# A transformer block on one core: the last block's end taken by quarters, tiles and two engines, score units by heads, and steps reordered at both ends

## The chip, the cores and the metric

One core of a Trainium2 chip runs the whole program. The metric is the device time of one execution in microseconds (us). TensorE (PE) multiplies matrices, VectorE (DVE), ScalarE (ACT) and GpSimd (POOL) work on tiles in SBUF and PSUM, and SyncE (SP) issues nearly all DMA transfers, in its own order.

## What is computed

A transformer block with adaptive norms over x of shape (8, 1024, 512), 16 heads of 32 columns, an MLP of width 2048, all in float32:

```python
mod = silu(condition) @ Wada + bada
sh_a, sc_a, gt_a, sh_m, sc_m, gt_m = split(mod, 6, axis=1)
xm = layernorm(x, g1, be1) * (1 + sc_a) + sh_a
x  = x + gt_a * (causal_attention(xm, Wqkv) @ Wproj + bproj)
xm = layernorm(x, g2, be2) * (1 + sc_m) + sh_m
x  = x + gt_m * (gelu(xm @ W1 + b1) @ W2 + b2)
```

## The kernel before, in words

The 8 x 1024 tokens are 16 blocks of 512 (two for each sequence); block n is the even or odd half of sequence n // 2. Two streams of work are merged into each engine's queue by a planner written in Python, which runs when the program is built and keeps a clock for each engine (`now`, L94), the time at which each value is ready (`written`) and the time at which each buffer is free (`left`).

The **attention stream** is `attend()` (L1392). For block n and each group g of 4 heads it runs *weight units* (`weights_T` L1282: transposed scores less the row maximum on PE into the PSUM tile "st", exponent on ACT L1317, on POOL the causal select L1322; then `weigh` L1334, the product with v, L1345) and, for the group that follows, *score units* (`scores` L1196: scores on PE into the same "st", L1208, causal mask L1220 and row maxima L1228 on DVE). An even block has 3 weight and 3 score units a group, an odd one 7 and 7. The exponents are added up in place over a group on POOL (L1429). `finish` (L1355) sums them over partitions by a matmul (L1363), copies the sums (L1369), takes their reciprocals on DVE in four parts (L1378) and divides on POOL (L1383). With the last group of a block this sets "attended" for it.

The **linear stream** is a generator that runs the steps of `plan` (L228 to L264) in order: k, q, v (projections for later blocks), "proj" (output projection, `project_out` L844), "mt" (norm, modulation and transposes ahead of the MLP, `modulated` L579), u (four up parts), d (four down parts, `down` L914; part 0 to 3 hold 2, 2, 1 and 2 products). Products are done by Strassen-like schemes with weight sums that are made once at the start: for W1 and W2 by `preparation()` (L670), stage by stage, four loads, four in-place additions on DVE or POOL (`either`, L148), four stores. "proj" of block n waits for "attended" n; "mt" is started as a side thread beside the main one. `work()` (L1106) advances the thread that can go soonest, the first of equals, side threads standing ahead of the main one:

```python
def threads():
    return sides + ([main] if main[0] is not None else [])
...
    advance(min(threads(), key=lambda thread: wait_of(thread[1])))
```

`step_aside` (L1135) stands ahead of each attention unit: it lets linear work in while that unit would have to wait, or while linear work is behind its share (`stream`). DVE work that isn't urgent (reciprocals, norm statistics) lies in `jobs`, and work that needs another ACT table (the norm's root and scaling L552 to L569, the gelu L871) in `excursions`; these run at set places of `attend`, or when `work()` finds every thread blocked.

Weights come through a ring of 9 tiles (`fetch`, L321), loaded by SP in the order in which the plan uses them; loads of x (L1035), gate rows (L489) and stores (L911) are issued in the same queue.

At the end (window 16, L264) the plan is: load x, down part 2 of block 14, proj 15, down part 3 of block 14, mt 15, and the MLP of block 15. The last down part of block 15 has its two products, then gate (POOL or DVE), addition and the two stores.

Of the kernel before, what the change touches and what calls it, by code (L numbers as in the profile page):

```python
# [22 lines left out]
def kernel(  # L23
# [123 lines left out]

    def either(out, a, b, op, reads, writes):  # L148

        n = 1  # L150
        for d in out.shape[1:]:
            n *= d
        on_dve, on_pool = 60 + 1.24 * n, 120 + 2.28 * n
        t = due(reads, writes)
        if max(now["DVE"], t) + on_dve + 1500 < max(now["POOL"], t) + on_pool:
            nc.vector.tensor_tensor(out, a, b, op)  # L156
            note("DVE", on_dve, reads, writes, port=True)
        else:
            nc.gpsimd.tensor_tensor(out, a, b, op)
            note("POOL", on_pool, reads, writes)  # L160
# [64 lines left out]
    def mlp_steps(n):  # L225
# [7 lines left out]
        + [("mod", 3), ("at", 2), ("v", 1), ("mod", 4), ("k", 2), ("gates", "m"), ("columns_m",)],  # L233
    }
    late = []
    for w in range(1, NB):
# [7 lines left out]
        if w == NB - 1:  # L244
            steps = late + [("load_xr", n)] + rows_a + [("proj", n), ("v", w)]
            steps += [("mt", n)] + rows_m + own + m[3:6]
# [17 lines left out]
    plan[NB] = [("load_xr", n), late[0], ("proj", n), late[1], ("mt", n)] + mlp_steps(n)  # L264
# [21 lines left out]
    def pieces_of(step):  # L286
# [4 lines left out]
        if kind == "gates":  # L291
            return [(Wada, GATES[step[1]][0], kh, fh) for kh, fh in RAW]
        if kind == "proj":
# [225 lines left out]
    def excursion(job, first=False):  # L519
        if alone[0]:  # L520
            job()
        else:
            excursions.insert(0 if first else len(excursions), job)

    def run_excursions(limit=None):
        n = len(excursions) if limit is None else min(limit, len(excursions))
        for _ in range(n):
            excursions.pop(0)()
# [4 lines left out]
    def normalize(tiles, key, sources):  # L533
# [8 lines left out]
        def statistics(t):  # L542
# [4 lines left out]
            if t == NTT - 1:  # L547
                excursion(root)
                excursion(apply)
# [26 lines left out]
        for t in range(NTT):  # L576
            add_job(lambda t=t: statistics(t), [sources[t]], key[0] == "m")

# [52 lines left out]
    def accumulate(pairs, reads=()):  # L631
        yield reads, [BANK]
        bank = lin_bank()
        for i, (lhsT, rhs) in enumerate(pairs):
            if i:
                yield [], []
            matmul(banks[bank], lhsT, rhs, i == 0, i == len(pairs) - 1, reads, bank)
# [32 lines left out]
    def preparation():  # L670

        for w in (W1, W2):
            for i in range(NQ):
                stage = act.tile([P, NC, TB], F32, tag="hT", name=f"prep_{LABEL[id(w)]}_{i}", bufs=NQ)
                got = {}
                for j, kf in enumerate(RAW):
                    a = next(a for a in ("A11", "A12", "A21", "A22") if FULL[a] == kf)
                    got[a] = stage[:, j, :]
                    nc.sync.dma_start(
                        got[a].rearrange("p (k n) -> p k n", n=HB), quarter(w, i, *kf)  # L680
                    )
                ready = now["PE"] + 12000
                for out, a, b, op, name in IN_PLACE:
                    yield ready
                    keys = [("prep", w is W2, i, a), ("prep", w is W2, i, b)]
                    either(got[out], got[a], got[b], op, keys, [("prep", w is W2, i, out)])
                    keep(w, i, name, got[out])
# [3 lines left out]
    def run_preparation(everything=False):  # L691
        while prepared[0] is not None:
# [4 lines left out]
            try:  # L697
                prepared[0][1] = next(prepared[0][0])
            except StopIteration:
                prepared[0] = None  # L700

# [142 lines left out]
    def project_out(n):  # L844
        at = take(NC)
        yield [("attended", n)], []
        attT = qTs.pop(n)
        tiles = [residual[n][:, t, :] for t in range(NTT)]
        for t, xt in enumerate(tiles):
            xt_job = lambda t=t, xt=xt: add_to(xt, gate_rows["gba"], [("row", "gba")], [("xr", n, t)])  # L850
            pool_jobs.append((xt_job, [("xr", n, t)]))
        for t, xt in enumerate(tiles):
            bank = yield from accumulate(
                [(attT[:, c, ts(t, P)], piece(at[c])) for c in range(NC)], [("att", n)]
            )
            tag, bufs = ("hat", NTT) if n == NB - 1 else ("y", 2)
            y = tmp.tile([P, D], F32, tag=tag, name=f"y_{n}_{t}", bufs=bufs)
            ky = ("y", n, t) if n == NB - 1 else y_key("proj", True)
            combine_out(y, bank, banks[bank], gate_rows["ga"], [("row", "ga")], [ky], ALU.mult)
            add_to(xt, y, [ky], [("xr", n, t)])  # L860
        release(*at)
        run_pool_jobs(True)
        normalize(tiles, f"m{n}", [("xr", n, t) for t in range(NTT)])

    def up(step):
# [11 lines left out]
        def finished():  # L877
            if q == NQ - 1:
                written["m used", n] = 0.0
            excursion(gelu, first=True)  # L880

        if (n, q) == (0, 0):
            run_preparation(True)
# [30 lines left out]
    def down(n, part):  # L914
# [40 lines left out]

        def stage(kind, tag, bufs=1):
# [37 lines left out]
        else:  # L994
# [6 lines left out]
            store(n, 1)  # L1001
            bank, ps = yield from product("B21")
# [9 lines left out]
    def perform(step):  # L1012
# [28 lines left out]
        elif kind == "at":  # L1041
            n = step[1]
            guards = [("m used", n - 3)] if n > 2 else [("v done", 0)] if n == 2 else []
            start(modulated(f"a{n}", *columns_of["a"], blocks[n][0], guards))
        elif kind == "sums":
# [12 lines left out]
        elif kind == "preps":  # L1058
            prepared[0] = [preparation(), 0.0]
        elif kind == "rows":  # L1060
# [45 lines left out]
    def work():  # L1106

        if linear_wait() == NEVER:
            run_jobs(True)
            run_excursions()  # L1110
        assert linear_wait() < NEVER
# [23 lines left out]
    def step_aside(reads, writes):  # L1135


        while threads():
            own, other = wait_of((reads, writes)), linear_wait()
# [56 lines left out]
    def scores(n, g, parts):  # L1196
# [5 lines left out]
        reads = [("qT", n), ("kT", n - h + parts[0][1])]  # L1202
        step_aside(reads, ["st"])
# [28 lines left out]
        if units[unit_at[0] + 1 :] == [] or units[unit_at[0] + 1][:2] != (n, g):  # L1232
            split_maxima(n, g, h)
# [121 lines left out]
    def finish(n, g):  # L1355
# [24 lines left out]

        def quotient():
            invert(3)
            nc.gpsimd.tensor_tensor(qTs[n][:, g, :], top, rec, ALU.mult)  # L1383
            note("POOL", 1285, [kr, "top"], [("att", n)])
# [7 lines left out]
    def attend():  # L1392
        previous = None
        for n in range(NB):
# [5 lines left out]
            for g in range(NC):  # L1400
                nxt = groups.index((n, g)) + 1
                for k in range(n_slots):
                    upto = len(units)
                    if nxt < len(groups):
                        lo, m = first_unit[groups[nxt]], len(score_units(*groups[nxt]))
                        upto = lo + min(m, -(-(k + 2) * m // n_slots))
                        if k == n_slots - 1 and nxt + 1 < len(groups):
# [6 lines left out]
            for g, k, upto in slots:  # L1414
# [9 lines left out]
                if k > 0:  # L1424
                    acc, first = totals[n, g]
                    for _, c0, w in parts:
                        for j in range(HPG):
                            into = acc[:, j, TB - w :]
                            nc.gpsimd.tensor_tensor(into, into, pT[:, j, c0 : c0 + w], ALU.add)  # L1429
# [113 lines left out]
```

## Time and profile before

| what | us |
|---|---|
| median of the runs | 3678.65 (3678.53 to 3679.02) |
| profiled execution, its own time | 3678.31 |
| its span, first to last instruction | 3676.6 |
| PE busy | 3575.4 (97%) |
| DVE busy | 2158.9 (59%) |
| POOL busy | 2044.1 (56%) |
| ACT busy | 1327.8 (36%) |

Busy time of PE counts a matmul as long as it takes, so work at a lower clock counts more. A line of a timeline has start, length, engine, source line, operation, tile written<-tiles read, shape and count; in brackets the idle time of the engine before it and what ended that. In a list of waits the three numbers are us in total, times, and the longest. Numbers after L are lines of the kernel before.

### The profile page before, as it was taken

To read this page: it belongs to the slowest core of one execution; us is meant where nothing else is said; L and a number is where in the kernel's file an instruction comes from. 1 tells how busy PE (TensorE), PEld (TensorE's weight loads), DVE (VectorE), ACT (ScalarE), POOL (GpSimd) and SP (SyncE) were. 2 spreads that over 40 slices of the span, in tenths; PEclk is the share of its full clock that TensorE was granted. 3 is DMA by queue.
4 is the path that set the end of the run, shared out by engine and by line. 5 is a ranking of instruction groups with operands and counts; after the bars stand their busy time and mean duration, and the time that the engine had idled before them with its cause. 6 is when DMAs were issued, how large, how long until landed. Compare 5 with 4: busy or idle time off the path is not lost.

```text
span 3676.6 us, 121132 instructions
## 1 busy us (share of the span) xinstructions
PE 3575.4 (97%) x54821; PEld 1767.9 (48%) x54821; DVE 2158.9 (59%) x2447; ACT 1327.8 (36%) x1412; POOL 2044.1 (56%) x2064
## 2 busy tenths in 40 slices
PE   8889999999999999999999999999999999998989
PEld 4424445445554455544445454444544445454445
DVE  5756675564746557465565666646666465654542
ACT  2334334252333523335242452424425144341421
POOL 3576645656455663566536665356653556444661
PEclk9989999999999999999999999999999999999999
DMA  6633333433333343433434333343333433333334
GB/s 208 195 118 99 119 94 107 126 103 122 112 110 118 105 125 111 139 96 97 125 108 136 97 98 119 113 132 101 102 119 111 134 104 113 105 106 122 89 111 133
DMA packets 307893, 430.34 MB, mean 117 GB/s; under 512 B 25900, under 2 KB 176236, under 8 KB 307380
## 3 DMA queue, kind: packets, MB, share of 16 engines
q1 hardware_dynamic: 307264, 422.56, 38.1%
q8 instruction: 432, 7.08, 0.8%
q14 instruction: 81, 0.66, 0.1%
q10 hardware_dynamic: 116, 0.03, 0.0%
HBM read 394.12 MB, written 28.38 MB: 115 GB/s over the span
## 4 chain that ended last, share of the span: by engine, by line
PE 86%; DVE 7%; ACT 2%; POOL 2%; issue 2%; DMA 0%; SPq 0%; ACTq 0%; POOLq 0%; DVEq 0%
PE bank L199 58%; PE st L1294 8%; PE sc L1208 8%; PE po L1345 7%; DVE mx L1228 2%; PE st L1305 2%; PE bank L1363 2%; POOL pT L1429 1%; PE bank L606 1%; ACT pT L1317 1%; DVE hT L929 1%; DVE sc L1220 1%; DVE xr L156 1%; DVE t_m L156 1%; PE bank L1268 0%
## 5 line engine op out<-in xcount | busy, mean ns | idle before, releaser
L1429 POOL TENSOR_TENSOR pT<-pT,pT 128x512 f32<-128x512 f32 (+3 forms) x1280 | 1207.8, 979 | 548.7 <-ACT pT L1317 382.4
L1317 ACT ACTIVATE pT<-st 128x2048 f32<-128x2048 f32 (+1 forms) x320 | 546.4, 1708 | 1020.1 <-PE st L1305 972.5
L199 PE MATMUL bank<-w,hT 128*32 128x256 f32 x14336 | 808.7, 380 | 4.9 <-DVE hT L929 2.1
L1228 DVE TENSOR_REDUCE mx<-sc 128x4 f32<-128x2048 f32 (+3 forms) x384 | 668.9, 1756 | 205.4 <-PE sc L1208 198.7
L199 PEld LDWEIGHTS bank<-w,hT 128*32 128x32 f32 x14336 | 453.2, 110 | 357.8 <-issue 61.3
L199 PE MATMUL bank<-xm_m,w 128*32 128x256 f32 x8192 | 506.5, 380 | 0.5 <-DVE u_u L191 0.5
L1322 POOL TENSOR_SCALAR_AFFINE_SELECT pT<-pT 128x512 f32<-128x512 f32 x256 | 177.8, 706 | 576.2 <-ACT pT L1317 575.9
L199 PE MATMUL bank<-t_m,w 128*32 128x256 f32 x6144 | 383.1, 380 | 2.4 <-DVE t_m L625 1.0
L1294 PE MATMUL st<-qT,kT 32*128 32x512 f32 (+3 forms) x3072 | 343.0, 531 | 37.1 <-DVE mx L1228 35.8
L199 PEld LDWEIGHTS bank<-xm_m,w 128*32 128x32 f32 x8192 | 254.3, 110 | 248.9 <-issue 95.8
L1208 PE MATMUL sc<-kT,qT 32*128 32x512 f32 (+3 forms) x3072 | 340.2, 527 | 10.5 <-DVE mx L1228 5.8
L1345 PE MATMUL po<-pT,v 128*32 128x512 f32 (+3 forms) x3072 | 315.6, 498 | 6.5 <-POOL pT L1322 6.5
L1220 DVE TENSOR_TENSOR sc<-sc,mask 128x512 f32<-128x512 f32 (+1 forms) x192 | 167.9, 875 | 251.2 <-PE sc L1208 223.0
L199 PEld LDWEIGHTS bank<-t_m,w 128*32 128x32 f32 x6144 | 193.0, 110 | 174.3 <-issue 50.2
L199 PE MATMUL bank<-w,qT 128*32 128x512 f32 x2048 | 243.1, 602 | 6.1 <-POOL qT L1383 3.2
L199 PE MATMUL bank<-xm_a,w 128*32 128x256 f32 x3968 | 243.1, 381 | 0.0
L1378 DVE RECIPROCAL rec<-rec 128x128 f32<-128x128 f32 x256 | 223.6, 917 | 21.0 <-ACT rec L1369 21.0
L1294 PEld LDWEIGHTS st<-qT,kT 32*128 32x128 f32 x3072 | 129.5, 185 | 202.0 <-issue 60.7
L1208 PEld LDWEIGHTS sc<-kT,qT 32*128 32x128 f32 x3072 | 126.8, 184 | 175.0 <-ACT pT L1317 84.7
L191 DVE TENSOR_TENSOR hT<-bank,u_u 128x512 f32<-128x512 f32 x192 | 130.3, 686 | 120.4 <-PE bank L199 118.4
L199 PE MATMUL bank<-t_a,w 128*32 128x256 f32 x2944 | 186.6, 382 | 0.0
L1317 ACT ACT_TABLE_LOAD x88 | 112.9, 1283 | 183.2 <-PE st L1305 182.5
(184 smaller groups left out, 3552.9 us busy)
## 6 DMA issues: line engine op xcount, KB each, us to landing
w<-in_L_cond_W_dram SPq DMA_DIRECT2D x384, 256.0 KB, 2.9
w<-kept_up_S SPq DMA_DIRECT2D x256, 256.0 KB, 2.6
w<-kept_down_S SPq DMA_DIRECT2D x256, 256.0 KB, 2.7
w<-kept_qkv_S SPq DMA_DIRECT2D x180, 256.0 KB, 2.9
w<-in_L_cond_Wqkv_dram SPq DMA_DIRECT2D x147, 256.0 KB, 3.5
hat<-in_x_dram SPq DMA_DIRECT2D x64, 256.0 KB, 3.5
w<-in_L_cond_Wproj_dram SPq DMA_DIRECT2D x64, 256.0 KB, 3.5
xr<-in_x_dram SPq DMA_DIRECT2D x64, 256.0 KB, 4.5
```

The source lines that it names most:

```text
L156: nc.vector.tensor_tensor(out, a, b, op)
L191: nc.vector.tensor_tensor(out, src, other, op)
L199: nc.tensor.matmul(ps[r, :], lhsT[:, r], rhs, start=start, stop=stop, skip_group_check=True)
L1208: nc.tensor.matmul(sc[:, j, c0 : c0 + w], qTs[n][r, g, ts(qt, P)], keys_of(n, kh)[r, g, :w], start=True, stop=True, skip_group_check=True,)
L1220: nc.vector.tensor_tensor(diagonal, diagonal, mask[:, :span].unsqueeze(1).to_broadcast([P, HPG, span]), ALU.add,)
L1228: nc.vector.tensor_reduce(mx[:, kh, qt, :], sc[:, :, c0 : c0 + w], axis=AX.X, op=ALU.max)
L1294: nc.tensor.matmul(st[:, j, c0 : c0 + w], kT[r, g, ts(k % NTT, P)], qT[r, g, TB - w :], start=(c0 == 0), stop=False, skip_group_check=True,)
L1317: nc.scalar.activation(pT[:, :, :used], st[:, :, :used], AF.Exp, scale=scale)
L1322: nc.gpsimd.affine_select(diagonal, diagonal, pattern=[[0, HPG], [1, P]], compare_op=ALU.is_ge, fill=0.0, base=0, channel_multiplier=-1,)
L1345: nc.tensor.matmul(po[r, TB - w :], v[:, k % NTT, g * P + j * hd : g * P + (j + 1) * hd], pT[:, j, c0 : c0 + w], start=(k == 0), stop=last ...
L1378: nc.vector.reciprocal(some, some)
L1429: nc.gpsimd.tensor_tensor(into, into, pT[:, j, c0 : c0 + w], ALU.add)
```

## The change

It touches the first blocks, the last two and the planner:

- *Score units by heads.* If linear work is more than 3 us away, no linear bank is in use, and "st" would be free over 1 us later than a bank, a score unit runs in the three linear PSUM banks, heads 0 to 2 first, then head 3, with masks and maxima head by head.
- *Order of the attention stream at block 0.* In the last group of block 0, score units for block 1 are held back: none after the first slot, at most one after the second; in the last slot one score unit runs, the group is closed at once, and the rest of the score units follow.
- *`hurry()`.* `step_aside` runs jobs and excursions whose inputs are due within 0.5 us as soon as every linear thread is blocked.
- *Preparation* loads one stage ahead; the first up step waits for "prepared" where it used to force what was left.
- *Plan.* In window 0 the columns of the MLP norm come ahead of k 2 and the MLP gates behind it. In window 15: down part 1 of block 13, load x, proj 14, mt 14, down parts 2 and 3 of block 13, v 15 (before: all three down parts, load x, proj 14, v 15, mt 14). In window 16 down part 3 of block 14 is a side thread, started ahead of proj 15.
- *Last group.* Additions of exponents for heads 1 and 3 go to DVE. The quotient is taken on DVE by quarters, each as soon as its reciprocal is there; that of the group before goes to DVE whole.
- *Last projection and norm.* The first two tiles start on three of their four pieces; each tile waits for its own quarter; residual, statistics, root and scaling are done tile by tile.
- *Last product.* The last product of the last down part runs one token tile after the other, in two banks; the rest of the sum is gated and added before; each tile is gated and added on DVE and stored.
- After the attention stream, `either` prefers DVE without its margin of 1500.

The core of the diff:

```diff
-        + [("mod", 3), ("at", 2), ("v", 1), ("mod", 4), ("k", 2), ("gates", "m"), ("columns_m",)],
+        + [("mod", 3), ("at", 2), ("v", 1), ("mod", 4), ("columns_m",), ("k", 2), ("gates", "m")],
...
-            steps = late + [("load_xr", n)] + rows_a + [("proj", n), ("v", w)]
-            steps += [("mt", n)] + rows_m + own + m[3:6]
+            steps = late[:1] + [("load_xr", n)] + rows_a + [("proj", n), ("mt", n)] + late[1:]
+            steps += [("v", w)] + rows_m + own + m[3:6]
...
-    plan[NB] = [("load_xr", n), late[0], ("proj", n), late[1], ("mt", n)] + mlp_steps(n)
+    plan[NB] = [("load_xr", n), late[0], ("beside", late[1]), ("proj", n), ("mt", n)] + mlp_steps(n)
...
+    def hurry():
+
+        while jobs and due(jobs[0][1]) <= now["PE"] + 500:
+            jobs.pop(0)[0]()
+        while excursions and due(excursions[0][1]) <= now["PE"] + 500:
+            excursions.pop(0)[0]()
...
+        load(*todo.pop(0))
+        while loaded:
+            if todo:
+                load(*todo.pop(0))
+            w, i, got, ready = loaded.pop(0)
...
+        for t, xt in enumerate(tiles):
+            if last:
+                while len(begun) <= max(t, 1):
+                    yield from begin(len(begun))
+                bank = begun[t]
+                yield [("att", n, t)], []
+                matmul(
+                    banks[bank], attT[:, NC - 1, ts(t, P)], piece(at[NC - 1]), False, True,
+                    [("att", n, t)], bank,
+                )
...
+            if last:
+                run_pool_jobs(True)
+                nc.vector.tensor_tensor(xt, xt, y, ALU.add)
+                note("DVE", 700, [ky, ("xr", n, t)], [("xr", n, t)], port=True)
+                following = normalize_tile(xt, f"m{n}", t, ("xr", n, t))
+                if t > 0:
+                    pending()
+                pending = following
...
-            run_preparation(True)
+            yield ["prepared"], []
...
+            for m in range(2):
+                yield [(n, "B21")], [BANK]
+                bank = lin_bank()
...
+                y = tmp.tile([P, HB], F32, tag="y", name=f"y_last_{m}")
+                nc.vector.tensor_tensor(y, banks[bank][:, :HB], gate, ALU.mult)
+                nc.vector.tensor_tensor(xr[:, m, c], xr[:, m, c], y, ALU.add)
...
+                nc.sync.dma_start(out[b, r0 : r0 + P, :], xr[:, m, :])
...
+        if (
+            linear_wait() > 3000
+            and not any(live)
+            and wait_of((reads, ["st"])) > wait_of((reads, [BANK])) + 1000
+        ):
+            scores_by_heads(n, g, parts, mx, reads)
+        else:
+            scores_at_once(n, g, parts, mx, reads)
...
+        if (n, g) == groups[-1]:
+            for i in range(NTT):
+                invert(i)
+                some = slice(i * part, (i + 1) * part)
+                nc.vector.tensor_tensor(qTs[n][:, g, some], top[:, some], rec[:, some], ALU.mult)
...
+                        if (n, g) == (0, NC - 1) and k < n_slots - 1:
+                            upto = lo + k
...
+                            if j % 2 and (n, g) == groups[-1]:
+
+                                nc.vector.tensor_tensor(into, into, pT[:, j, c0 : c0 + w], ALU.add)
...
+                if (n, g, k) == (0, NC - 1, n_slots - 1):
+
+                    next_scores()
+                    close(*previous)
+                    previous = None
```

## The prediction, made before the result was known

> **What bounds the kernel now.** I read the page's slices first, then the busy time by stretch, then who waited for whom inside the stretches that stand out, then the timeline of each.
>
> ```profile
> PE   8889999999999999999999999999999999998989
> ...
> PEclk9989999999999999999999999999999999999999
> ```
>
> TensorE is at nine tenths or more in 35 of 40 slices. It can be gained on only in the first three slices and in the fourth and second from the end, and the granted clock is lower in the third slice too. I cut the span there (columns: stretch, length, busy us and count of PE, PEld, DVE, ACT, POOL, then granted clock, DMA share, GB/s):
>
> ```profile
> 172.00:211.60 39.60, 22.23 (x157) 6.54 (x160) 20.54 (x21) 8.31 (x7) 27.46 (x31) 0.70 0.50 167
> ...
> 256.00:282.00 26.00, 18.59 (x136) 6.09 (x136) 14.68 (x14) 12.77 (x13) 13.85 (x11) 0.80 0.00 1
> 282.00:3331.00 3049.00, 3019.02 (x46436) 1497.93 (x46432) 1820.01 (x2049) 1143.62 (x1212) 1709.56 (x1730) 1.00 0.38 113
> 3331.00:3350.00 19.00, 16.16 (x144) 4.61 (x140) 2.67 (x4) 0.00 (x0) 6.29 (x5) 0.91 0.62 200
> 3350.00:3385.00 35.00, 27.25 (x368) 12.40 (x360) 19.09 (x27) 13.20 (x16) 14.57 (x21) 0.95 0.29 89
> ...
> 3514.00:3544.00 30.00, 21.14 (x276) 9.18 (x269) 18.23 (x17) 5.26 (x5) 24.45 (x23) 0.98 0.33 102
> ...
> 3669.30:3676.60 7.30, 0.00 (x0) 0.00 (x0) 0.69 (x1) 0.00 (x0) 2.52 (x2) 0.70 0.22 84
> ```
>
> Length minus PE busy is PE's idle time: A (172 to 211.6) 17.4 us, B (256 to 282) 7.4, C (3331 to 3350) 2.8, D (3350 to 3385) 7.75, E (3514 to 3544) 8.9. The 3049 us between B and C hold only 30. Work done at half clock costs more: the stretches granted 0.50 hold 15.65 us of PE work in A, 8.45 in B, 3.27 in C, 3.21 in D, 2.86 in E, and half of each is lost: 7.8, 4.2, 1.6, 1.6, 1.4. So the stalls cost A 25.2, B 11.6, C 4.4, D 9.4, E 10.3: 61 us, plus the tail after the last matmul.
>
> Who PE waited for in A and B, then in the middle:
>
> ```profile
> PE st L1294 <- DVE mx L1228: 16.0, 6, 4.7
> PE sc L1208 <- DVE mx L1228: 5.8, 2, 3.4
> ```
> ```profile
> PE st L1294 <- DVE mx L1228: 14.3, 30, 0.9
> ```
>
> Scores and exponent units share one PSUM tile ("st"), so each waits out the other's DVE or ACT pass. That costs nothing while linear work (projections, MLP) fills the gap; in A and B there is none. In A the next step, block 0's output projection, needs "attended", whose quotient ends at 208.3; in B the next is the MLP norm of block 0, ready at 274.7.
>
> **The change part by part.**
>
> *Start (A, B).* Today five score units of block 1 are queued between the first and second weight unit of the last group of block 0, and two more before the third (seven units at 143.5 to 176). The change leaves only the two already done, puts one between, closes the group, then runs the other six. The second weight unit follows the first (151.1) after its exponent, about 155.5; the third about 159.5. POOL then sets the end: selects 1.2+0.6, additions 5.9+2.8, a quotient 1.3 and perhaps one preparation group 5.4, from 158, give 169.5 to 175; matmul and copies 2; reciprocals 3.4, with up to one 2.3 reduction ahead; quotient 1.3. So "attended" falls at 178 to 183, take 181, instead of 208. Linear work left after 153.7 is 12.9 us, attention 8.5: PE runs dry at about 175. By 181 PE has done what the old program had done at 172 plus 2.6; of A's 22.2-7.8=14.4 us of work 11.8 remain, and they now lie beside 12 us of projection and 12 of the q step. The old state of 211.6 is reached at 192.8: 19 gained, 15 if "attended" comes at 185. I take 17.
> Score units by heads use three free linear banks instead of "st". Nearest row: a 128x512 maximum is 0.68 us, so four are 2.7 against 2.29 for one of 128x2048; PE does two passes for one, 1.1 us more. They are taken only if linear work is over 3 us away: a cost of 0.4 DVE inside a gap, against waits of 2.4 to 4.7 us. Zero net if seldom taken, up to 2 us a unit if often; counted in A and B.
> B: the norm's square root and scaling now run as soon as the planner finds no linear work, and the q step (12 us) with six score units covers the norm. B's 11.6 shrinks to about 3.6: 8 gained. It needs the preparation of weight sums done by about 212. Today its last group ends at 251.2; loading one stage ahead moves each group up by one or two places (the group before ended 219.5, the one before that 198.4), so 200 to 215. Late by 5 us, B gains 3. Price on SP: four more 256 KB loads in flight, about 2 us of issue in front of weight loads, hidden by the nine-deep ring; if not, 2 us lost. Moving the gate step behind the k step moves its four weight loads, two bias loads and two stores too, and 2.3 us of DVE column work (176.7 to 179) out of A.
>
> *Last window (C, D).* C is a DMA queue:
>
> ```profile
> 3339.03 0.43 SPq L489 DMA_DIRECT2D row_ga<-kept_ga  x1
> ...
> 3343.98 1.29 DVE L191 TENSOR_TENSOR y<-bank,row_ga 128x512 f32<-128x512 f32 x2 [11.64 <-DMA row_ga<-kept_ga]
> ```
>
> The gate row is issued behind the previous block's stores (3335.1) and four loads (3.0 us). With the projection moved ahead of the last two down parts, those stores come later: row issued some 3 us after the projection starts, landed at 8 to 9, needed at 10.5 (three banks of 3.5). C gains 4 (2 if a value kept in one of two "y" buffers makes outputs go singly). D: the norm gets 20.7 us of down work and 12 of v to hide its additions and statistics; only root and scaling remain, since excursions run when no linear work is left, at about 3362 instead of 3367.6 to 3380.7. D gains 5 (2 to 8); the 2.17 wait for the diagonal's maximum stays.
>
> *Attention's end (E).*
>
> ```profile
> 3502.60 11.91 POOL L1429 TENSOR_TENSOR pT<-pT,pT 128x512 f32<-128x512 f32 x8
> ...
> 3532.65 0.64 PE L1345 MATMUL po<-pT,v 128*32 128x256 f32 x8 [2.26 <-POOL pT L1322]
> ...
> 3538.04 3.39 DVE L1378 RECIPROCAL rec<-rec 128x128 f32<-128x128 f32 x4 [3.77 <-ACT rec L1369]
> ...
> 3541.60 1.49 POOL L1383 TENSOR_TENSOR qT<-top,rec 128x512 f32<-128x512 f32 x1 [5.38 <-DVE rec L1378]
> ...
> 3543.14 2.79 PE L199 MATMUL bank<-w,qT 128*32 128x512 f32 x12 [3.25 <-POOL qT L1383]
> ```
>
> POOL is full from 3500 to 3536. Waits for it are 1.69+0.37+0.72+2.26+0.49=5.5, then 3.25 for the quotient. Half the additions go to DVE. [...] The last quotient by quarters gives the first at 0.9+0.2 (128x128: between 0.16 and 0.69, take 0.2) instead of 3.4+1.5, and the projection starts on three quarters of its sum early: 3.25 gone.
> But the down part that hid the norm (3555.7 to 3569.6) becomes a side thread, and the planner takes side threads before the main one when both are ready, so it is spent before the projection. What is late next is the norm, by tiles: from the last projection matmul, output 0.25+0.69, addition 0.8, statistics 1.0, root 0.5, reciprocal and offset 0.5, scaling 0.8, transposes 0.6, two evacuations 1.1: 6.3, less 1.4 of transposes: 4.9 idle. [...]
>
> *Tail.*
>
> ```profile
> 3669.36 0.69 DVE L191 TENSOR_TENSOR y_d<-bank,u_d 128x512 f32<-128x512 f32 x1 [6.21 <-PE bank L199]
> 3670.13 1.26 POOL L159 TENSOR_TENSOR y_d<-y_d,row_gm 128x512 f32<-128x512 f32 x1 [2.85 <-DVE y_d L191]
> 3671.47 1.26 POOL L159 TENSOR_TENSOR xr<-xr,y_d 128x512 f32<-128x512 f32 x1
> ```
>
> From matmul's end to the store 3.4 us. By tiles: two DVE operations of 128x256, about 0.38 each (half of 0.69 and a fixed part; 0.69 at most), and one store instead of two (0.4 less). The first tile and the sum of the earlier parts lie beside matmuls. 2.9 gained (2 to 3.2).
>
> *Middle.* The 30 us there could lose 14.3 to units by heads, or grow where the planner decides otherwise: -10 to +12, taken as 0.
>
> Sum: 17+8+4+5+3+2.9=39.9. The profiled execution took 3678.3 (span 3676.6 and 1.7 around it), the median of the runs is 3678.65: 3639.
>
> **Rivals.**
> Start stays bound by POOL and DVE: additions and reductions keep "attended" past 195 and the preparation is late. For it: POOL 27.5 of 39.6 us busy in A; against: the five units out of the way. A 6, B 0: gain 21, 3658.
> Everything closes: middle waits too (10 of 14.3) and the last projection goes ahead of the side thread (5 more): 3624. Against: linear work is seldom 3 us away there.
> Slower: table loads. Excursions run early cost ACT two table loads of 1.28 each; there are 90 visits (60 and 30). If each held an exponent so that PE lost 0.55, 49.5 us are lost against 40 won: 3688. It decides from 0.44 a visit. Against: ACT is busy 36%, and PE waits for it under 5 us in the middle.
> It doesn't do what it says: the moved units and the new order only move the stalls, gain under 7: about 3676.
>
> **Numbers.** Forecast 0.58, start stays 0.18, everything closes 0.12, only moved 0.05, slower 0.07. A measurement here tells about 0.2% (7 us) from no change. Faster 0.88, same 0.05, slower 0.07. The range, from term bounds and the neighbouring cases, is 3620 to 3660.
>
> **What would show it.** Right: block 0's projection at about 181 to 185; few waits of st for mx before 220; no gap at row_ga; one gap of about 5 us after the last projection; one DVE pair between last matmul and store. Wrong: idle time after 300 above 35 us, more table loads, or a stall for the preparation before the first up step.

## The result, and the profile after

The changed kernel takes 3650.88 us (median, 3647.89 to 3653.37) against 3678.65 (3678.16 to 3680.71) beside it: ratio 0.9923 [0.9911, 0.9934], 27.8 us gained where 39.7 were forecast, inside the range. Measured again later it took 3649.79, ratio 0.9918 [0.9904, 0.9931]. The profiled execution took 3647.89 us, its span 3646.2. Numbers after L are now lines of the changed kernel: the matmul L199 is L201, the maximum L1228 is L1392, the exponent units' scores L1294 are L1456, the last reciprocals L1378 are L1540, the quotient L1383 is L1557; units by heads are L1343 (scores) and L1359 (maxima). The lines of an experiment's trace have the numbers of its own kernel.

The page's busy time of PE, its slices and the granted clock:

```profile
PE 3571.6 (98%) x54821; PEld 1770.1 (49%) x54821; DVE 2179.1 (60%) x2501; ACT 1329.2 (36%) x1413; POOL 2014.6 (55%) x2039
...
PE   8999999999999999999999999999999999999999
...
PEclk9999999999999999999999999999999999999999
```

Only the first slice is left below nine tenths. The same stretches as before (A, B, the middle, C, D, E), columns as in the prediction:

```profile
172.00:211.60 39.60, 31.61 (x196) 10.59 (x198) 31.07 (x37) 5.42 (x5) 22.37 (x20) 0.70 0.50 161
256.00:282.00 26.00, 25.82 (x358) 11.37 (x358) 17.67 (x16) 8.17 (x7) 17.94 (x14) 1.00 0.35 113
282.00:3331.00 3049.00, 3019.55 (x46328) 1494.75 (x46324) 1815.18 (x2055) 1141.82 (x1207) 1715.56 (x1735) 1.00 0.37 113
3331.00:3350.00 19.00, 17.43 (x271) 9.75 (x260) 7.31 (x12) 7.47 (x10) 9.08 (x14) 0.93 0.70 223
3350.00:3385.00 35.00, 34.71 (x443) 15.16 (x445) 20.57 (x20) 13.17 (x13) 18.35 (x17) 0.94 0.19 57
3514.00:3544.00 30.00, 23.28 (x228) 9.97 (x221) 26.23 (x44) 6.91 (x12) 12.60 (x11) 0.91 0.34 106
```

Idle time of PE in A is 8.0 instead of 17.4, in B 0.2 instead of 7.4, in C and D together 1.9 instead of 10.6; the middle holds 29.5 as before. By this cut the start has won some 17 us. It has not, and the cut can't tell: the same stretch of time holds other work in the two kernels. What tells it is how much earlier the same work comes. The down parts run the same 14336 matmuls (bank<-w,hT) in every kernel here. The table has the time at which 500, 1500 and 10000 of them are through (the start of the next one), the start of the v step of block 2, which may not begin before block 1's attention is through, and the span's end. The first row is in us from the span's start, the others are us earlier than before, one profiled execution each; the experiments named are described below, and e14_again is the changed kernel a second time:

| kernel | output projection of block 0 starts | first up part starts | 500 | v of block 2 starts | 1500 | 10000 | end |
|---|---|---|---|---|---|---|---|
| before (us) | 211.5 | 280.3 | 403.3 | 442.0 | 640.4 | 2842.2 | 3676.6 |
| changed | 13.1 | 23.8 | 13.6 | 10.6 | 11.0 | 13.9 | 30.4 |
| e14_again | 13.6 | 23.4 | 13.2 | 9.1 | 9.5 | 11.2 | 30.0 |
| e1_recips_at_once | 38.8 | 50.7 | 51.6 | 6.7 | 5.6 | 7.2 | 23.0 |
| e10_recips_k3 | 38.2 | 52.4 | 53.3 | 9.2 | 17.3 | 19.6 | 36.8 |
| e2_no_heads | 13.3 | 28.8 | 27.5 | -0.7 | -2.1 | -1.1 | 14.6 |
| e3_end_only | 1.3 | 15.4 | 7.6 | 4.6 | 4.7 | 5.4 | 22.8 |
| e13_start_only | 11.1 | 19.5 | 9.3 | 6.3 | 6.7 | 8.5 | 4.5 |

The seven traces of kernels with the changed start (changed, e14, e4 to e7, e13) have 6.7 to 11.0 us at 1500, so a difference of a few us between two rows says nothing.

And PE's idle time plus half of its busy time under a granted 0.50, by stretch of the trace (half is near what is lost: in the changed kernel eight score matmuls of 32x512 take 1.14 us at 172.32, at the full clock, and 2.09 at 195.97, at 0.50):

| kernel | to 500 us | 500 to 3300 | from 3300 to the last matmul |
|---|---|---|---|
| before | 45.5 + 12.0 | 26.7 + 0 | 21.8 + 4.7 |
| changed | 37.2 + 8.9 | 22.8 + 0 | 10.4 + 5.4 |
| e14_again | 36.7 + 13.1 | 22.4 + 1.7 | 10.6 + 2.5 |
| e1_recips_at_once | 42.3 + 9.5 | 22.6 + 1.6 | 10.5 + 5.8 |
| e10_recips_k3 | 34.3 + 4.5 | 23.5 + 0 | 10.5 + 4.4 |
| e2_no_heads | 48.4 + 14.3 | 24.0 + 1.7 | 10.7 + 5.7 |
| e3_end_only | 42.0 + 11.1 | 25.3 + 0 | 10.6 + 4.0 |
| e13_start_only | 38.3 + 11.5 | 22.5 + 1.7 | 24.3 + 8.8 |

The changed kernel's first row: 11.4 us gained to 500, 3.9 in the middle, 10.7 from 3300 and 3.2 in the tail, 29.2 of the spans' 30.4 (its second trace: 7.7, 2.6, 13.4 and 3.2). The forecast had 25, 0, 12 and 2.9. Its start is what fell short.

Why A's end came late is in the timelines of DVE and POOL of the changed kernel (start, length, engine, line):

```profile
177.87 0.93 DVE L1540 RECIPROCAL rec<-rec 128x128 f32<-128x128 f32 x1
...
185.02 0.94 DVE L1540 RECIPROCAL rec<-rec 128x128 f32<-128x128 f32 x1
...
190.87 0.94 DVE L1540 RECIPROCAL rec<-rec 128x128 f32<-128x128 f32 x1
...
195.83 0.94 DVE L1540 RECIPROCAL rec<-rec 128x128 f32<-128x128 f32 x1
```
```profile
196.94 1.49 POOL L1557 TENSOR_TENSOR qT<-top,rec 128x512 f32<-128x512 f32 x1 [3.98 <-DVE rec L1540]
```

The sum of exponents was there at 172.4 (its matmuls start at 170.9, forecast 169.5 to 175). But the four reciprocals, 3.7 us of work, are spread over 19: one is let through after one or two score units, and DVE takes their masks and maxima in between.

### The profile page after: what moved, and what is told of

Same layout as the page of the kernel before. It is cut to its first block, busy times and chain, and to the rows that moved or that the text cites. A ratio compares the mean times of both kernels' runs of the same rounds, so it can differ in the third digit from the quotient of the medians.

```text
span 3646.2 us, 121167 instructions
## 1 busy us (share of the span) xinstructions
PE 3571.6 (98%) x54821; PEld 1770.1 (49%) x54821; DVE 2179.1 (60%) x2501; ACT 1329.2 (36%) x1413; POOL 2014.6 (55%) x2039
## 5 line engine op out<-in xcount | busy, mean ns | idle before, releaser
L1611 POOL TENSOR_TENSOR pT<-pT,pT 128x512 f32<-128x512 f32 (+3 forms) x1266 | 1189.2, 973 | 524.9 <-ACT pT L1479 377.1
L201 PE MATMUL bank<-w,hT 128*32 128x256 f32 x14336 | 808.6, 380 | 2.8 <-DVE hT L1006 2.1
L1392 DVE TENSOR_REDUCE mx<-sc 128x4 f32<-128x1024 f32 (+3 forms) x381 | 664.4, 1757 | 192.4 <-PE sc L1372 185.8
L201 PEld LDWEIGHTS bank<-w,hT 128*32 128x32 f32 x14336 | 452.1, 110 | 354.0 <-issue 58.0
L201 PE MATMUL bank<-xm_m,w 128*32 128x256 f32 x8192 | 506.6, 380 | 0.6 <-ACT rec L1531 0.5
L201 PE MATMUL bank<-t_m,w 128*32 128x256 f32 x6144 | 383.2, 380 | 0.9 <-ACT hT L188 0.9
L201 PEld LDWEIGHTS bank<-xm_m,w 128*32 128x32 f32 x8192 | 253.3, 110 | 252.0 <-issue 98.0
L1456 PE MATMUL st<-qT,kT 32*128 32x512 f32 (+3 forms) x3072 | 339.6, 526 | 21.0 <-DVE mx L1392 20.0
L1372 PE MATMUL sc<-kT,qT 32*128 32x256 f32 (+3 forms) x3048 | 340.6, 527 | 2.9 <-DVE mx L1392 1.9
L1384 DVE TENSOR_TENSOR sc<-sc,mask 128x1024 f32<-128x1024 f32 (+1 forms) x191 | 166.7, 873 | 248.5 <-PE sc L1372 225.5
L201 PEld LDWEIGHTS bank<-t_m,w 128*32 128x32 f32 x6144 | 191.9, 110 | 175.7 <-issue 54.2
L201 PE MATMUL bank<-xm_a,w 128*32 128x256 f32 x3968 | 243.5, 381 | 0.0
L201 PE MATMUL bank<-w,qT 128*32 128x512 f32 x2048 | 241.1, 597 | 0.4 <-DVE qT L1547 0.2
L1540 DVE RECIPROCAL rec<-rec 128x128 f32<-128x128 f32 x256 | 224.6, 919 | 8.5 <-ACT rec L1531 8.5
L1456 PEld LDWEIGHTS st<-qT,kT 32*128 32x128 f32 x3072 | 128.9, 184 | 182.7 <-issue 57.5
L201 PE MATMUL bank<-t_a,w 128*32 128x256 f32 x2944 | 187.2, 382 | 0.0
```

Of the source, the lines that this page charges most:

```text
L201: nc.tensor.matmul(ps[r, :], lhsT[:, r], rhs, start=start, stop=stop, skip_group_check=True)
L1372: nc.tensor.matmul(sc[:, j, c0 : c0 + w], qTs[n][r, g, ts(qt, P)], keys_of(n, kh)[r, g, :w], start=True, stop=True, skip_group_check=True,)
L1384: nc.vector.tensor_tensor(diagonal, diagonal, mask[:, :span].unsqueeze(1).to_broadcast([P, HPG, span]), ALU.add,)
L1392: nc.vector.tensor_reduce(mx[:, kh, qt, :], sc[:, :, c0 : c0 + w], axis=AX.X, op=ALU.max)
L1456: nc.tensor.matmul(st[:, j, c0 : c0 + w], kT[r, g, ts(k % NTT, P)], qT[r, g, TB - w :], start=(c0 == 0), stop=False, skip_group_check=True,)
L1540: nc.vector.reciprocal(some, some)
```

## The experiments

Each edit is made on the changed kernel. "Before" was run beside each: 3680.53 us beside e1 to e4, 3679.75 beside e5, e6, e10 and e11, 3679.84 beside e7, e13, e14 and e15. Kernels from different groups are best compared by their ratios.

### The start: is the late projection what was lost?

**e1_recips_at_once.** The reciprocals and the quotient of block 0's last group are issued at once, not as jobs:

```diff
+        if (n, g) == (0, NC - 1):
+            for i in range(3):
+                invert(i)
+            quotient()
+            return
```

> The changed kernel (median 3650.9) with the four reciprocals and the quotient of block 0's last group issued at once after its sum, ahead of the score units that follow. Theory 1 (queue order): 'attended' of block 0 came at 198.4 instead of the forecast 181 because the planner lets one reciprocal through between two score units (177.9, 185.0, 190.9, 195.8), each behind 3 to 4.6 us of maxima on DVE. Then the quotient ends at 181 to 183, the projection starts there, most of the 8.0 us of idle time and 8.9 us of half-clock loss between 172 and 200.6 go, and the time falls by 8 to 13 us, to 3638 to 3643. Rival (DVE is simply full, 25.8 of 28.6 us): the 3.7 us of reciprocals only push the six score units back, block 1's first weight unit comes that much later, and the time changes by less than 3 us: 3648 to 3653.

3653.53 us, ratio 0.9929 [0.9917, 0.9942]: no faster than the changed kernel. Yet the edit did all that it should: the four reciprocals run as one piece from 172.63 to 176.02, the projection starts at 172.7, the first up part 27 us before the changed kernel's, and the 500th down matmul comes 51.6 us before its old time. By the 1500th, 5.6 are left. The theory that the late quotient costs the missing time fell. Where the time went back is in the windows of 380 to 440 us, first e1's, then the changed kernel's:

```profile
380.00:440.00 60.00, 43.66 (x504) 17.70 (x496) 32.57 (x46) 19.40 (x17) 45.33 (x52) 0.89 0.12 40
```
```profile
380.00:440.00 60.00, 55.62 (x880) 28.71 (x872) 39.73 (x39) 17.14 (x15) 48.10 (x41) 1.00 0.34 101
```

16.3 us idle instead of 4.4, a lower clock, and hardly any transfers of weights (40 GB/s). PE's timeline of e1 shows the stall of A once more, 220 us later:

```profile
392.75 2.09 PE L1456 MATMUL st<-qT,kT 32*128 32x512 f32 x8 [3.31 <-DVE mx L1392]
...
416.85 0.62 PE L1430 MATMUL bank<-ident_b,mcols 128*32 128x128 bf16 x16 [5.04 <-DVE mcols L1414]
...
435.29 1.07 PE L201 MATMUL bank<-w,xm_a 128*32 128x256 f32 x16
```

From 387 to 435 no linear matmul runs; scores and exponent units alternate on "st" alone, and pay for each other's passes in full. The first linear matmul after it is v of block 2. By the plan this step may not start before block 1's attention is through with its buffers ("free for v"), and it stands next in the list, behind block 0's last down parts, so everything after it waits too. Linear work done earlier is linear work that is missing here. The rival's mechanism shows as well: block 1's first exponent unit starts at 206.4 instead of 196.0, and v of block 2 at 435.3 instead of 431.4. In the table every kernel but e10 has kept at 1500, within 1.4 us, just what it has gained by the start of this v step, whatever it had gained at 500: the gate's opening sets what stays of the start.

**e10_recips_k3.** If that is so, work that can be released in that stretch brings the gain back. k of block 3, 12 us of matmuls, needs only the k buffer of block 0, which is free after block 1's last full exponent unit on it:

```diff
+            if w == 2:
+                steps = late + [("k", 3), ("v", 2), ("load_xr", n), ("proj", n)]
...
-            written["free for k", n + 2 if n % 2 else n + 1] = 0.0
+            if n != 1:
+                written["free for k", n + 2 if n % 2 else n + 1] = 0.0
...
+                if (n, g, k) == (1, NC - 1, NTT - 1):
+                    written["free for k", 3] = 0.0
```

> Block 0's last reciprocals at once, as in e1_recips_at_once, and in addition the k step of block 3 goes ahead of the v step of block 2, from the moment block 1's last full exponent unit has read the buffer that it takes. Theory (a stall is not removed but moved: in e1_recips_at_once TensorE starts early on the linear work and has none left at 389 to 434, because the next step in the list is the v step of block 2, which may not start before block 1's attention is through): 12 us of work become available in that stretch, some 8 of its 16 us of idle time and 2 of lost clock go, time 3643.5. Rival (attention itself, paced by VectorE, sets the end of that stretch, and what is filled there is missing after block 2): idle time moves on to a later place, time 3653 as in e1_recips_at_once.

3645.19 us, ratio 0.9906 [0.9893, 0.9920]; its window:

```profile
380.00:440.00 60.00, 52.35 (x752) 24.24 (x748) 35.99 (x47) 21.77 (x19) 43.76 (x50) 1.00 0.24 76
```

8.7 us of e1's 16.3 idle us are gone and the clock stays full, as expected (8 and 2). At the 1500th matmul it is 11.7 us ahead of e1, at the 10000th 12.4: filled for good, not passed on to a third place; the medians show 8.3.

**e11_k3.** The same order of k and v without the reciprocals:

> The changed kernel with only the k step of block 3 ahead of the v step of block 2. Its idle time from 380 to 440 is 4.4 us, against 16.3 in e1_recips_at_once, so by the theory of the moved stall this order alone brings at most 2 us: 3649 to 3651. If it brings as much as in e10_recips_k3 (over 5 us), the order is good by itself and says nothing on where the start's gain went.

3650.39 us, ratio 0.9922 [0.9908, 0.9935], the changed kernel's time. So neither half does it: the reciprocals at once bring nothing alone, nor does k 3; together 5 to 6 us.

**e14_again and e15_k3_again.** The changed kernel and e10's once more, on one chip.

> The changed kernel itself once more, to stand beside the next three on one chip. Expected as first measured, 3651, ratio 0.9923; what it differs by is what a difference between two calls is worth.

> The kernel of e10_recips_k3 again, now on one chip with the changed kernel. Theory (the moved stall was filled for good): 5 to 6 us faster than the changed kernel beside it, 3645. Rival (the difference between the two earlier calls): within 2 us of it, 3650.

3649.79 (3648.28 to 3652.11) and 3644.40 (3642.9 to 3646.2), ratios 0.9918 [0.9904, 0.9931] and 0.9903 [0.9888, 0.9918]. The intervals of the ratios overlap because before's own runs spread over 7 us; the runs of the two kernels don't. 5.4 us, as expected: this version beats both kernels.

**e2_no_heads.** Units by heads never taken:

```diff
-            linear_wait() > 3000
+            False
```

> The changed kernel with score units by heads never taken. The trace of the changed kernel has two such units, both between 177 and 192, each with about 4.7 us of masks and maxima on DVE where a unit at once has 3.0, and two PE passes for one. Theory 1: they are not what carries the change; without them DVE has 3 us less to do ahead of the last reciprocals, but the shared tile is waited for again: within 2 us of 3650.9. Rival (they carry the gain of the start): 5 us or more slower, 3656 or above. Second rival (they are what makes DVE late): 3 to 6 us faster, 3645 to 3648.

3663.37 us, ratio 0.9951 [0.9938, 0.9963]: some 11 us lost (0.0028 to 0.0033 of the time, by the two ratios of the changed kernel) by a part that the prediction took as zero. PE's window of 380 to 440 again:

```profile
380.00:440.00 60.00, 50.35 (x669) 21.92 (x669) 28.29 (x27) 17.25 (x14) 51.25 (x50) 0.87 0.22 72
```

Without them PE turns to linear work sooner (first up part 5 us ahead of the changed kernel's) and attention is behind: v of block 2 starts at 442.7 instead of 431.4. From 418 to 443 no linear matmul runs, and the 27.5 us at 500 turn into -2.1 at 1500. So the two units by heads, at 177 to 192, bring block 1's attention to its end some 11 us sooner; that this is because they use a stretch in which PE has nothing else fits the traces and is not shown apart.

### How much is the start worth by itself, and the end?

**e3_end_only.** The start as before (order of units, no units by heads, preparation, place of the columns step); early work (`hurry`) and the end as changed:

```diff
-                        if (n, g) == (0, NC - 1) and k < n_slots - 1:
-                            upto = lo + k
...
-                if (n, g, k) == (0, NC - 1, n_slots - 1):
-
-                    next_scores()
-                    close(*previous)
-                    previous = None
...
-            yield ["prepared"], []
+            run_preparation(True)
```

> The changed kernel with the start as before: the score units not held back, the group not closed early, no units by heads, preparation loaded stage by stage and forced by the first up step, the norm columns behind the gates. The early running of jobs and excursions stays, and all of the last two windows and the end. Theory 1: the gain of the start was 11 us (shift of like waits at 938 us) and that of the end 16: 3661 to 3664. Rival (the early running of jobs, not the order of units, makes the start's gain): 3651 to 3655.

3655.49 us, ratio 0.9932 [0.9919, 0.9944]: 25.0 us gained without the start's parts, where the changed kernel has 27.8; 4.7 of them are there by the 1500th matmul, so from the early work. Beside e2, run on the same chip, it is 7.9 us faster. So the start's other parts (order of units, early closing, preparation, place of the columns) lose time as long as the units by heads are not there, and the start pays through these units.

**e13_start_only.** The reverse: the start and the early work as changed, the end (plan of the last windows, additions, quotient, norm, projection, last product) as before.

```diff
-        last = n == NB - 1
+        last = False
...
-        if (n, g) == groups[-1]:
+        if False:
...
-    margin[0] = 0
     run_excursions()
-    run_jobs(True)
-    written["attended", NB - 1] = 0.0
```

> The start as changed (order of units, early closing, units by heads, preparation one stage ahead, early work when nothing linear is at hand), the end all as before: order of the last windows, norm, quotient, additions and last product. Theory (by the trace of the changed kernel, 13.9 us are gained by 2830 us into the span, and start and end do not touch): 3666, and a gain that makes up the changed kernel's with the end's 15 to 17. Rival (by e3_end_only, the end and the early work alone bring all but 3 us, so the start is worth little by itself): 3673.

3673.97 us (3670.4 to 3674.96), ratio 0.9983 [0.9974, 0.9992]: 5.9 us gained; the theory of 3666 fell, the rival's 3673 held, but not for its reason alone. The start did gain 8.5 by the 10000th matmul; half of that was lost again at the end. Its window of attention's end, its waits of PE there, and two rows of POOL:

```profile
3500.00:3540.00 40.00, 22.72 (x180) 7.78 (x176) 10.43 (x10) 10.80 (x8) 34.43 (x35) 0.72 0.03 9
```
```profile
PE po L1505 <- POOL pT L1482: 8.1, 3, 4.7
PE st L1454 <- ACT pT L1477: 6.0, 2, 4.9
PE bank L201 <- POOL qT L1555: 3.3, 1, 3.3
```
```profile
3504.97 10.71 POOL L1609 TENSOR_TENSOR pT<-pT,pT 128x512 f32<-128x512 f32 x8
...
3516.36 4.93 POOL L1609 TENSOR_TENSOR pT<-pT,pT 128x512 f32<-128x512 f32 x4
```

17.3 us idle at a granted 0.72, and 9 GB/s: the down parts that lay beside the last group before (its last ones end at 3530.4) are used up at 3502.2, and PE then waits for POOL and ACT in full. The same thing as in e1, at the other end of the program. Start and end do touch, through the stock of linear work. Whether the new order or the early work uses it up is not separated; e13 has both.

### The parts of the end

**e4_proj_first.** Down part 3 of block 14 behind the last projection, not beside it:

```diff
-    plan[NB] = [("load_xr", n), late[0], ("beside", late[1]), ("proj", n), ("mt", n)] + mlp_steps(n)
+    plan[NB] = [("load_xr", n), late[0], ("proj", n), late[1], ("mt", n)] + mlp_steps(n)
```

> The changed kernel with the last plan as before: last output projection first, then the last down part of block 14 as a step of the main thread, so that it lies between the projection and the norm, as it did; quarters, tiles and two engines stay. The changed kernel has gaps of 2.26 and 2.10 us and 2.1 us of half-clock loss around the norm by tiles (3536 to 3545). Theory (as the prediction had it: the norm is uncovered because the down part is spent ahead of the projection): those go, and a wait for the first quarter of the quotient of 0 to 3 us comes: 3 to 6 us faster, 3645 to 3648. Rival (the wait for the last group's sum and quotient, now uncovered from 3520 to 3527, costs as much or more): 3650 to 3655.

3652.95 us, ratio 0.9923 [0.9910, 0.9937], no clear difference. The part covers either the additions or the norm, and the other stands bare (here PE waits 6.1 us for POOL's selects): 8.2 us idle from 3500 to 3560 against 6.7, at 0.89 against 0.94. The prediction's 5 us for this order are not there.

**e5_pool_adds.** All additions of the last weights on POOL:

```diff
-                            if j % 2 and (n, g) == groups[-1]:
+                            if False:
```

> The additions of block 7's last weights all on GpSimd again, everything else as changed. Theory (VectorE and GpSimd take turns at these additions, but VectorE's half still frees GpSimd for some 6 us, which the forecast set against 5.5 us of waits for GpSimd): TensorE waits for pT again near 3530, 4 us or more lost, time 3655. Rival (under turns nothing is saved, the last unit is as late either way): within 1 us of the changed kernel, 3651.

3652.04 us, ratio 0.9927 [0.9914, 0.9939]: 1 to 3 us lost, by the medians and by the ratios, against the changed kernel's two measurements, which differ by 1.1 themselves; nearer the rival (within 1) than the theory (4 or more). Its rows of POOL and PE's wait for the quotient:

```profile
3515.50 6.45 POOL L1611 TENSOR_TENSOR pT<-pT,pT 128x384 f32<-128x384 f32 x8
...
3522.61 2.78 POOL L1611 TENSOR_TENSOR pT<-pT,pT 128x256 f32<-128x256 f32 x4
```
```profile
PE bank L201 <- DVE qT L1547: 2.8, 1, 2.8
```

POOL's last addition ends at 3525.4 instead of 3520.5, 4.9 us later where the theory had some 6 by an estimate of the author's, but the down part and the projection's first three pieces lie beside it, so that PE waits 2.8 for the quotient instead of 1.57 for the sum and 0.25 for the quotient in the changed kernel. Where they don't lie there, as in e13, PE waits over ten us for what the same additions hold up.

The turns are in the traces. In the kernel before, POOL and DVE start additions in alternation, at 3510.02, 3511.09, 3512.25 and 3513.30: POOL's two of 128x512 take 2.28 and 2.26 us, where the six ahead of them took 1.28 to 1.30, and DVE's two of 128x1024 take 2.29 each. In the changed kernel POOL's two of 128x512 at 3506.3 take 1.79 and 1.71 and DVE's two beside them 0.69 and 1.77; POOL's two ahead of them, with DVE idle, took 1.27 and 1.28.

**e6_old_window15.** The last window but one in its old order:

```diff
-            steps = late[:1] + [("load_xr", n)] + rows_a + [("proj", n), ("mt", n)] + late[1:]
-            steps += [("v", w)] + rows_m + own + m[3:6]
+            steps = late + [("load_xr", n)] + rows_a + [("proj", n), ("v", w)]
+            steps += [("mt", n)] + rows_m + own + m[3:6]
```

> The last window but one in its old order (last two down parts ahead of the projection), everything else as changed. Theory: the wait for the gate row behind the previous block's stores returns (4.4 us gained by the trace), and the norm loses its cover (4.2 gained): time 3659. Rival (the gaps only moved, and the two down parts are missing as cover in attention's end): less than 3 us lost, 3653.

3653.99 us (3647.53 to 3656.72), ratio 0.9929 [0.9917, 0.9942]: some 2 to 4 us, nearer the rival. In its trace the wait for the gate row is back, with 2.58 us of PE's time behind it, and idle time and half clock from 3300 are 20.3 instead of 15.8. D does not come back: the root and the scaling run early in both orders. The spread of this run is as large as the difference, so more than "at most a few us" isn't shown.

**e7_old_tail.** The last product for both tiles at once:

```diff
-            if n == NB - 1:
-                yield from last_product(u3, next_pieces=[next(at) for _ in range(NQ)])
-                return
```

> The last product by the old way (one product of both tiles, difference and scaling and addition after it, two stores), everything else as changed. Theory (after the last matmul, 7.3 us before and 4.1 in the changed kernel's trace): 3 us slower than the changed kernel, 3654. Rival (the tail's start lay in the shadow of the last stores and only moved): 3651.

3650.73 us, ratio 0.9919 [0.9906, 0.9933], 0.9 us from the changed kernel beside it. The last rows of DVE show why not 3:

```profile
3644.08 0.69 DVE L158 TENSOR_TENSOR y_d<-y_d,row_gm 128x512 f32<-128x512 f32 x1
3644.80 0.69 DVE L158 TENSOR_TENSOR xr<-xr,y_d 128x512 f32<-128x512 f32 x1
```

With `margin` at zero the planner puts these two on DVE, 0.69 each, where POOL took 1.26 each before. From the last matmul to the end of the span: 7.3 before, 6.1 here, 4.1 changed. So 1.1 us of the tail's 3.2 belong to `margin`, and 2 us to the tiles in this trace; the medians show 0.9 of them.

## Why the prediction was right in sign and range, and short in size

- *Order of the weight units and the sum*: right (152.3, 155.9 and 159.5 for the units, 170.9 for the sum). One reading behind it was off: before, three score units ran between the first and second weight unit (154.7 to 162.3), not five; the two others ran ahead of the first.
- *"Attended" at 178 to 183*: wrong, 198.4. The failed step is "reciprocals 3.4, with up to one 2.3 reduction ahead". `hurry` runs a job when its inputs are due, and each reciprocal writes the "rec" that the next one reads; so, by the code, one is due at a time, and at least one score unit lies between any two.
- *"17 gained" and "8 gained"*: this step failed most. 6.7 to 11.0 of the 25 are there at the 1500th matmul, and e1 shows that the late reciprocals are not why: with the quotient as early as forecast, 5.6 are there. The sum took time gained by 282 us as kept, since the middle held only 30 idle us. But the plan lets no linear work through between the last down part of block 0 and the end of block 1's attention, at about 430; what PE did sooner it lacked there. With a step let past that gate (e10) 17.3 are kept. The rival "only moves the stalls", taken at 0.05, had the mechanism; the changed kernel lies between it and the forecast. The rival "start stays bound" had one sign right, "attended" past 195, but not its cause: the sum and the preparation were on time.
- *Preparation done by 212, B closed to 3.6*: the preparation was right, the last of its additions on POOL starts at 200.1. B's stretch of time holds 0.2 us idle at a full clock, but that is the cut which can't tell what is kept.
- *Units by heads, "zero net"*: mis-sized. The one with the causal mask costs DVE 4.7 us in this trace (four masks of 0.42, four pairs of maxima of 0.76) against 3.6 for the same unit on "st" (1.23 and 2.36), so 1.1 more where 0.4 was taken, and only two units are done so. Still e2 puts the part at some 11 us of gain. Without it the time is 3663.37, outside the range: that the range held owes something to luck.
- *C and D, "4" and "5"*: idle time 8.7 us less in the trace, close to the sum. Put back alone (e6) the old order costs only 2 to 4; D's gain is there without the new order.
- *E, "3"*: no run shows this term, which rested on the author's estimate of what the two engines and the clock would leave beside the norm's 4.9; in its place the trace has 1.5 by the same sum. PE's waits for POOL are down to 1.57, the quotient's 3.25 to 0.25, and the norm's gaps stand bare as forecast (4.9 taken, 0.18+2.26+2.10+0.23 = 4.8 found):

```profile
3536.26 0.33 PE L641 MATMUL bank<-ident,xh_m 128*128 128x128 f32 x1 [0.18 <-ACT xh_m L608]
...
3538.85 0.48 PE L641 MATMUL bank<-ident,xh_m 128*128 128x128 f32 x1 [2.26 <-ACT xh_m L608]
...
3541.43 0.48 PE L641 MATMUL bank<-ident,xh_m 128*128 128x128 f32 x1 [2.10 <-ACT xh_m L608]
```

With half clock on 4.1 us of work it is 8.8 instead of 10.3. Taken together the end's parts were costed well against the old start: e3, which has it, is at 14.6 us of idle time and half clock from 3300, 11.9 below before, and its tail has the same 3.2; the forecast had 12 and 2.9. Against the new start, where e13 is at 33.1 and the changed kernel at 15.8, they are worth 17.3 and 3.2: some 5 us of their value lie in what the new start, or the early work, would have broken. The additions on two engines, set against 5.5 us of waits, are worth 1 to 3 us at most here (e5).
- *Tail, "2.9"*: 3.2 by the trace, in DVE operations of 0.42 and 0.43 (0.38 estimated).
- *Slower: table loads*: refuted, 181 loads against 180.
- *The signs*: one sign of being wrong came: PE's idle time after 300 us is 39.9 us (51.7 before), above the 35 that was named. Of the signs of being right one failed: block 0's projection started at 198.4, not at 181 to 185.
- *Middle, "0"*: 3.9 less idle time between 500 and 3300 us. e13, with the old end, has 4.2 less. e3, which has the early work and the old start, has only 1.4 less, so the early work alone doesn't explain it; the cause stays open.

What stays open: how the 37.2 us idle before 500 split further (17.0 lie before 140, which nothing here touches), and a version without `hurry`, which the rest of the change leans on and which was not tried.

## What to carry to other kernels

Where two streams fill each other's waits, the work that fills is a stock, and time won by using it early is only a loan: find the next point at which the stock is shut off (here a buffer that one step waits for, with everything behind it in line), and count what is left at that point before and after. Measure a gain at like pieces of work further on, not by the idle time of the stretch that was changed. Parts that look idle alone may pay in pairs: the reciprocals brought nothing, the order of k and v nothing, both together 5.4 us.

## What the runs showed of the hardware

In the changed kernel a clock once halved stayed so under work:

```profile
176.40:200.30 23.90, 17.79 (x88) 6.82 (x84) 22.50 (x31) 2.30 (x2) 9.39 (x11) 0.50 0.67 216
```

For 23.9 us the granted clock was 0.50 while PE's records cover 74% of it, from 182.9 to 194.1 all but 0.6 us. From 182.9 to 189.2, 6.3 us without a gap in the records, of score matmuls with 32 rows, didn't bring the full clock back; it came back at 200.3, during the output projection. The number of matmuls doesn't tell the two cases apart. In the next two rows the first is of the changed kernel, 16 matmuls of 32 rows, with half clock before and after; the second is of the kernel before, 16 matmuls of 128 rows (the output projection) that cover less of the time, after which the full clock came back:

```profile
183.20:186.60 3.40, 3.40 (x16) 1.81 (x14) 3.31 (x8) 0.00 (x0) 0.00 (x0) 0.50 0.98 342
...
3542.60:3546.00 3.40, 2.86 (x16) 0.78 (x20) 1.72 (x2) 0.00 (x0) 3.40 (x4) 0.50 0.00 0
```

The two differ in the rows, in the time covered and in what went before; no run changed one of these alone, so what brings the clock back was not shown. Nor did the half clock come after long gaps alone. In the kernel before it was granted at 3344.6, 3371.9 and 3542.6, near the end of gaps of 2.85, 2.61 and 3.25 us; in the changed kernel it was granted at 3347.3 after three gaps of 0.38 to 0.44 us, with PE's records covering 2.1 of the 3.4 us before. Where the stall at the start is filled the loss goes with it: e10 has half clock for 6.8 us there instead of 23.9, and of the 7.3 us by which it beats the changed kernel's first trace before 500 us, 4.4 are clock and 2.9 idle time.
